# Eight chunks in four pairs: rescheduling a graph product and moving weight masks to GpSimd

## The chip, the core and the metric

The kernel runs on one core of a Trainium2 chip. The metric is the device time of one execution in microseconds (us); before the change three runs took 2383.52 to 2384.42, median 2384.4. Everything is computed in float32.

Five engines matter here: PE (TensorE, matrix products into PSUM), DVE (VectorE), ACT (ScalarE), POOL (GpSimd) and SP, which only issues DMAs. Each engine works through its own instructions in the order in which the program text gives them to it (the kernel runs under a manual schedule). An instruction that waits holds back all that stand behind it on its engine.

## What is computed

For each of 16 samples, layer 0 builds a weight matrix from the layer-normed sample, multiplies the sample with it (the graph product), and uses the result as queries of an attention. Layer 1 multiplies with a fixed normalised adjacency and applies two linear layers with batch norms.

```
h = max(layernorm(x), 0)                      # (16, 1024, 256)
A_s = 2*| |sigmoid(c_m - c_n) - 0.5| - 0.5 |  # c: channel mean of each node
g = relu((h^T @ (adj * A_s)) * para)          # graph product, 256 x 1024
k, v = split(h @ kv_w)
x = x + softmax(g^T k * scale) v              # 4 heads of 64
h = max(layernorm(x), 0)
agg = A_hat @ h;  z = relu(BN(agg @ W1.T + b1));  x = x + BN(z @ W2.T + b2)
```

The weight matrix is made from `1 - tanh(|.|)`: the kernel forms `w = (tanh(|row - col|) - 1) * adj` and puts the sign into a later scale.

## The kernel before

**Tiles.** The 1024 nodes of a sample are eight chunks of 128; each chunk `c` has a weight tile `ws[b, c]` of 128 x 1024. `differences(b, c)` (L349) makes its absolute value and tanh on ACT (L353, L356); `masked(b, c)` (L359) subtracts 1 and multiplies by `adj_t[c]` on DVE in one instruction (L361). The tiles come from pools: `w4` has five, `pp` has eight with the tag `p` (probabilities, and between attentions loaded tiles) and two with the tag `acc`, and `ow` has one each of the tags `sums` and `att`. A new tile of a full pool waits until its predecessor has been read for the last time.

**A sample's period.** For samples 2 to 15 the order is: attention of sample b (`attention`, L791), graph product and keys and values of sample b+1 (`graph_seven`, L501), then layer 1's first product of sample b (`linear1_all`). Samples 0 and 1 use the plain `graph` (L384).

**Attention.** Four steps, two heads over 512 queries each. In step s, `scores(s)` issues sixteen score products, eight exponentials on ACT and, on DVE, running sums of the probabilities (`acc`, `odd`; L816, L822, L825); then the steps in `before_last`, then the last sum (L830). `partial(s)` transposes and reduces the sum on DVE (L836, L844), and `values(s)` multiplies with `v` and transposes the output into `oT` (L865). The `hooks` fill `before_last`: in steps 0 and 1 the weight tiles 0 and 1 of the next sample. After `partial(2)`, `scale` of the first half (two of the four steps) multiplies `oT` by the reciprocals (L903), and SP issues sixteen DMAs (L920) that lay it out in the tile `att`. `add` (L928) adds `att` to half of the sample `x` on DVE. For the first half this call, `add0`, stands late in the graph product; the second half's `collect`, `invert`, `spread`, `scale`, `add1` are spread over the graph product and what follows.

**Graph product.** `graph_seven` treats chunks 0 and 1 plainly (`plain`, four block products of 128 x 128 by 128 x 512 for each chunk, L514) and the other six in three pairs. A pair's 2 x 2 by 2 x 2 block product takes seven products (`m1` to `m_7`, L575) instead of eight, with sums s1 to s4 of blocks of h on the left (made beforehand by `pair_sums`, stored by POOL's DMA queue, loaded again by SP at L527 and L528) and differences t1 to t4 of weight tiles on the right (`make_t1` to `make_t4`, one DVE instruction of 128 x 512 each, L556 to L568). The sum of several products stands in one PSUM tile `x` that is copied out three times in between (L642, L654, L659). t2 and t3 use the still empty `v` and `kT` tiles.

**Loads.** At the head of `graph_seven` SP loads the sums, h transposed (L532), `para` (L535) and, by `load_more`, the six tiles of the three adjacency differences that `linear1` reads (L982).

Of the kernel before, what the change touches and what calls it, by code (L numbers as in the profile page):

```python
# [10 lines left out]
F32 = mybir.dt.float32  # L11
# [6 lines left out]
P = 128  # L18
# [11 lines left out]
def fast_path(  # L30
# [37 lines left out]
    gs_d = [dram.tile([P, 12, P], F32, tag=f"fgs_{b}", name=f"fgs_{b}") for b in range(B)]  # L68
# [107 lines left out]
    with ExitStack() as stage:  # L176
# [181 lines left out]

        def masked(b, c):  # L359
            w = ws[b, c]  # L360
            nc.vector.scalar_tensor_tensor(w, w, 1.0, adj_t[c], ALU.subtract, ALU.mult)  # L361
# [100 lines left out]
        PLAIN = 2  # L462
        PAIRS = (NC - PLAIN) // 2

        def h_pairs(b, n0, n1):

            view = hs[b][:, PLAIN + 2 * n0 : PLAIN + 2 * n1, :].rearrange(
                "p (n k) c -> p n k c", k=2
            )
            return lambda i, k: view[:, :, k, ts(i, P)]  # L470
# [30 lines left out]
        def graph_seven(b, left, norm, load_more, last):  # L501
# [5 lines left out]
            add0, collect, invert, spread, scale, add1 = left  # L507
            h = hs[b]

            def plain(c):  # L510
                w = ws.pop((b, c))
                for d in range(CC):
                    for g in range(NH):
                        nc.tensor.matmul(  # L514
                            gps[d][:, ts(g, 512)],
                            h[:, c, ts(d, P)],
                            w[:, ts(g, 512)],
                            start=(c == 0),
                            stop=(c == PLAIN - 1),
                        )  # L520


            w7 = pp.tile([P, N], F32, tag="acc", name=f"f_w_{b}_7", bufs=2)
            rest = pp.tile([P, 2, 512], F32, tag="acc", name=f"f_kt4_{b}", bufs=2)
            sums_h = ow.tile([P, 4, 2, P], F32, tag="sums", name=f"f_gs_{b}")
            sums_c = rest[:, 0].rearrange("p (s q) -> p s q", s=4)
            nc.sync.dma_start(sums_h, gs_d[b][:, 0:8].rearrange("p (s n) q -> p s n q", s=4))  # L527
            nc.sync.dma_start(sums_c, gs_d[b][:, 8:12])  # L528
# [7 lines left out]
            load_more()  # L536
# [6 lines left out]
            def s_of(q):  # L543
                return [sums_h[:, q, n] for n in range(2)] + [sums_c[:, q]]
# [3 lines left out]
            def part_w(n, k, j):  # L548
                return ws[b, PLAIN + 2 * n + k][:, ts(j, 512)]

            t2 = [diffs[:, 2 * n] for n in range(2)] + [room[:, 3]]
            t3 = [diffs[:, 2 * n + 1] for n in range(2)] + [room[:, 1]]
# [34 lines left out]
            def m2(n):  # L587
                one(c_of[0, 0], a(0, 1)[:, n], part_w(n, 1, 0), n)

            def m3(n):  # L590
                one(c_of[0, 1], s4[n], part_w(n, 1, 1), n)

            def m4(n):
                one(c_of[1, 0], a(1, 1)[:, n], t4[n], n)
# [10 lines left out]
            differences(b, 2)  # L605
            differences(b, 3)
            differences(b, 4)
            masked(b, 2)
            masked(b, 3)
            collect()  # L610
            invert()
            masked(b, 4)
            plain(0)
            differences(b, 5)
            make_t3(0)
            make_t1(0)
            make_t2(0)
            spread()
            masked(b, 5)
            plain(1)  # L620
            differences(b, 6)
            differences(b, 7, w7)
            m1(0)
            m2(0)
            make_t4(0)
            m3(0)
            m_7(0)
            m1(1)
            make_t3(1)
            masked(b, 6)  # L630
            m2(1)
            m4(0)
            m_7(1)
            m3(1)
            make_t1(1)
            make_t2(1)
            sums = big.tile([P, 2, 4, P], F32, tag="row", name=f"f_kvs_{b}")
            nc.sync.dma_start(sums.rearrange("p m n q -> p (m n) q"), kvs_d)
            scale()
            masked(b, 7)  # L640
            m1(2)
            nc.scalar.copy(room[:, 0], x)  # L642
# [3 lines left out]
            m2(2)  # L646
            m6(0)
            m6(1)
            make_t4(1)
            make_t4(2)  # L650
            m_7(2)
            m3(2)
            m6(2)
            nc.scalar.copy(room[:, 2], x)  # L654
            m4(1)
            m4(2)
# [3 lines left out]
            add0()  # L660
# [3 lines left out]
            t23 = ow.tile([P, 2, 512], F32, tag="att", name=f"f_kt23_{b}")  # L664
            kt2, kt3, kt4 = t23[:, 0], t23[:, 1], rest[:, 1]
# [9 lines left out]
            for d in range(CC):  # L675
                nc.vector.tensor_add(both(d), both(d), gps[d])
            for c in range(PLAIN, NC):
                ws.pop((b, c))
# [69 lines left out]
            arrive(b + 1)  # L748
            V.add(1, 0, 7)
# [41 lines left out]
        def attention(b, qT, kT, v, hooks):  # L791
# [4 lines left out]
            def scores(s, within=None, before_last=()):  # L796
                g, pair = steps[s]
                for m in range(NC):
                    ps = ps_s.tile([P, 2, 512], F32, tag="s", name=f"f_s_{b}_{s}_{m}")
                    for e in range(2):  # L800
                        rows_e = slice(e * HD, (e + 1) * HD)
                        nc.tensor.matmul(  # L802
                            ps[:, e, :],
                            kT[rows_e, pair, ts(m, P)],
                            qT[rows_e, pair, ts(g, 512)],
                            start=True,
                            stop=True,
                        )
                    p = pp.tile([P, 2, 512], F32, tag="p", name=f"f_p_{b}_{s}_{m}")
                    nc.scalar.activation(p, ps, AF.Exp)  # L810
                    p_of[s, m] = p
                    if m == 1:
                        acc = pp.tile(
                            [P, 2, 512], F32, tag="acc", name=f"f_acc_{b}_{s}", bufs=2
                        )
                        nc.vector.tensor_add(acc, p_of[s, 0], p)  # L816
                        acc_of[s] = acc
                    elif m == 3:
                        odd = ow.tile([P, 2, 16, 32], F32, tag="sums", name=f"f_sums_{b}_{s}")
                        odd_of[s] = odd  # L820
                        flat = odd.rearrange("p e j i -> p e (j i)")
                        nc.vector.tensor_add(flat, p_of[s, 2], p)  # L822
                    elif m > 3:
                        to = flat if m % 2 else acc_of[s]
                        nc.vector.tensor_add(to, to, p)  # L825
                    if m == 5 and within:
                        within()
                for step in before_last:
                    step()
                nc.vector.tensor_add(acc_of[s], acc_of[s], flat)  # L830

# [104 lines left out]
            for i in range(len(steps)):  # L936
                scores(
                    i,
                    collect if i == 2 else None,
                    [*hooks.get(i, ()), *([invert, spread] if i == 2 else [])],  # L940
                )
                partial(i)
                if i == 2:
                    scale()
                values(i)
            return [add] + finish(1)
# [31 lines left out]
        def load_thirds(b):  # L978
            made = [third_tiles(b, k) for k in range(3)]
            for k in range(3):  # L980
                for i in range(KH // 2):
                    nc.sync.dma_start(made[k][i], t_d[k][:, 2 * i : 2 * i + 2, :])  # L982
            return made
# [382 lines left out]
        with tc.manual_schedule(engines={ENG.PE, ENG.Activation, ENG.DVE, ENG.Pool, ENG.SP}):  # L1366
# [73 lines left out]
            for b in range(B):  # L1440

                hooks = {}
                if b + 1 < B:
                    for c in range(2):
                        hooks.setdefault(c, []).append(lambda c=c: weights(b + 1, c))
# [8 lines left out]
                left = attention(b, *qkv, hooks)  # L1454

                def more(c):
# [5 lines left out]
                        lambda: turn_h(b + 1), more(2), left[0], left[1], left[2], more(3),  # L1462
                        left[3], left[4], more(4),
# [4 lines left out]
                    4: [left[5], lambda: norm.stats(4, NC), norm.invert],  # L1468
# [8 lines left out]
                if b + 1 < B:  # L1477
                    more_loads = {}

                    def load_more():  # L1480
                        if 0 < b < B - 2:
                            more_loads["thirds"] = load_thirds(b)

                    if b == 0:
                        qkv = graph(b + 1, between)
                        todo = []
                    else:
                        qkv, todo = graph_seven(b + 1, left, norm, load_more, b + 2 == B)
                        thirds = more_loads.get("thirds")
# [4 lines left out]
                if b + 2 < B:  # L1494
                    made = None
                    if b > 0:
# [9 lines left out]
                        turning=lambda: (pair_sums(b + 2, 2, 3), turn_h_aside(b + 2)),  # L1506
# [5 lines left out]
                else:  # L1512
# [3 lines left out]
                    def first():  # L1516
                        norm.stats(0, 4)
                        norm.invert(0, 4)
                        left[3]()
                        left[4]()  # L1520
# [5 lines left out]
                    def third():  # L1526
                        left[5]()
# [17 lines left out]
                    for step in left[:3]:  # L1545
                        step()
# [897 lines left out]
```

## Time and profile before

The page describes one execution: its own time is 2382.97 us, of which 2381.1 are the span from first to last instruction.

| | before |
|---|---|
| median of three runs | 2384.4 us |
| the profiled execution | 2382.97 us |
| its span | 2381.1 us |
| PE busy | 2343.5 us, 98% |
| DVE busy | 1989.6 us, 84% |
| ACT busy | 1352.6 us, 57% |
| POOL busy | 175.1 us, 7% |
| granted PE clock, mean | 0.995 |
| one period (attention, graph product, layer 1), from the scores at 1111.45 to those at 1241.98 | 130.5 us |

Busy time is the union of an engine's instructions. A group line reads: line, engine, operation, output <- inputs, shapes, count | busy us, mean ns of one | idle time just before and what ended it. A float32 product appears as two PE records, and each record's own duration (592 ns) overlaps the next one's, so that PE advances faster than the mean suggests. The timeline merges neighbours: start in us, duration, engine, line, operation, count. Inside the loop PE is never idle by these records; its idle time lies at the start and at the end.

### The profile page before, as it was taken

How to read it: one execution, taken by the hardware profiler on the slowest of the kernel's cores; microseconds unless marked ns; L12 is line 12 of the kernel's file. 1: busy time of each engine (PE TensorE's matmuls, PEld its weight loads, DVE VectorE, ACT ScalarE, POOL GpSimd, SP SyncE). 2: the span in 40 equal slices, each digit the busy share in tenths (PEclk: the TensorE clock that was granted, in tenths of full speed). 3: DMA queues.
4: the chain of work that ended last, by engine and by line, in shares of the span. 5: the costliest groups of instructions: out<-in, count | busy, mean ns of one | idle time of the engine just before them, and what ended most of it. 6: DMA issues, size and time to landing. Idle time of an engine off the chain costs nothing.

```text
span 2381.1 us, 25131 instructions
## 1 busy us (share of the span) xinstructions
PE 2343.5 (98%) x8286; PEld 1037.3 (44%) x8286; DVE 1989.6 (84%) x2866; ACT 1352.6 (57%) x2002; POOL 175.1 (7%) x253
## 2 busy tenths in 40 slices
PE   8999999999999999999999999999999999999996
PEld 4443444434343434444343434344444434444444
DVE  6888989797989899897979798998979798757766
ACT  6846556464746555565647374555555575346654
POOL 2030010101010000101010100001010100000000
PEclk9999999999999999999999999999999999999998
DMA  5043433432342424334333414243433321355569
GB/s 194 8 145 93 147 119 129 137 122 91 97 160 68 167 93 169 97 129 137 124 98 110 146 62 169 89 172 93 146 120 127 114 92 53 114 203 188 175 238 381
DMA packets 178651, 316.40 MB, mean 133 GB/s; under 512 B 33616, under 2 KB 117072, under 8 KB 178512
## 3 DMA queue, kind: packets, MB, share of 16 engines
q1 hardware_dynamic: 164176, 271.18, 33.7%
q0 software_dynamic: 9728, 26.76, 3.8%
q10 hardware_dynamic: 4608, 16.78, 1.7%
q8 instruction: 67, 1.10, 0.2%
q14 instruction: 72, 0.59, 0.1%
HBM read 198.71 MB, written 97.05 MB: 124 GB/s over the span
## 4 chain that ended last, share of the span: by engine, by line
PE 97%; DVE 1%; DMA 1%; ACT 0%; issue 0%; SPq 0%; DVEq 0%; ACTq 0%; POOLq 0%; POOL 0%
PE f_s L802 19%; PE f_o L852 19%; PE f_aps L1011 16%; PE f_zps L1118 6%; PE f_gps L575 6%; PE f_gpsx L575 5%; PE f_gps L514 4%; PE f_zx L1661 4%; PE f_zm L1661 3%; PE f_gps L404 2%; PE f_kpsx L712 2%; PE f_vpsx L717 2%; PE f_vps L717 2%; PE f_kps L712 1%; PE f_z2ps L1599 1%; PE f_outps L1884 1%
## 5 line engine op out<-in xcount | busy, mean ns | idle before, releaser
L810 ACT ACTIVATE f_p<-f_s 128x1024 f32<-128x1024 f32 x512 | 477.5, 1048 | 189.2 <-PE f_s L802 189.1
L802 PE MATMUL f_s<-f_qT,f_kT 64*128 64x512 f32 x2048 | 457.3, 596 | 0.1
L852 PE MATMUL f_o<-f_p,f_v 128*64 128x512 f32 x2048 | 453.6, 595 | 0.0
L802 PEld LDWEIGHTS f_s<-f_qT,f_kT 64*128 64x128 f32 x2048 | 190.2, 185 | 264.8 <-ACT f_p L810 117.9
L852 PEld LDWEIGHTS f_o<-f_p,f_v 128*64 128x64 f32 x2048 | 141.4, 137 | 304.3 <-issue 265.4
L353 ACT ACTIVATE f_w<-f_row,f_col 128x1024 f32<-128x1024 f32 x127 | 147.0, 1157 | 40.0 <-PE f_gps L514 26.8
L825 DVE TENSOR_TENSOR f_acc<-f_acc,f_p 128x1024 f32<-128x1024 f32 x128 | 155.9, 1218 | 4.5 <-ACT f_p L810 4.5
L361 DVE SCALAR_TENSOR_TENSOR f_w<-f_w,f_adj 128x1024 f32<-128x1024 f32 x127 | 152.8, 1213 | 7.5 <-ACT f_w L356 7.2
L825 DVE TENSOR_TENSOR f_sums<-f_sums,f_p 128x1024 f32<-128x1024 f32 x128 | 155.8, 1217 | 0.0
L260 POOL TENSOR_TENSOR f_rstd_b<-f_var_b,f_mhalf 128x4 f32<-128x4 f32 (+1 forms) x31 | 33.1, 1069 | 1483.0 <-DVE f_var_b L259 1483.0
L356 ACT ACTIVATE f_w<-f_w 128x1024 f32<-128x1024 f32 x127 | 134.4, 1058 | 4.0
L1011 PE MATMUL f_aps<-f_ahatT,f_hs 128*128 128x512 f32 x256 | 115.1, 592 | 0.0
L1011 PE MATMUL f_aps<-f_ahatT,f_h_b 128*128 128x512 f32 x256 | 112.7, 593 | 0.0
L1011 PE MATMUL f_aps<-f_t,f_hs 128*128 128x512 f32 x256 | 112.5, 592 | 0.0
L816 DVE TENSOR_TENSOR f_acc<-f_p,f_p 128x1024 f32<-128x1024 f32 x64 | 76.9, 1201 | 27.6 <-ACT f_p L810 27.5
L514 PE MATMUL f_gps<-f_w,f_h_a 128*128 128x512 f32 x224 | 99.9, 599 | 0.0
L822 DVE TENSOR_TENSOR f_sums<-f_p,f_p 128x1024 f32<-128x1024 f32 x64 | 78.3, 1223 | 21.8 <-ACT f_p L810 21.8
L281 ACT ACTIVATE f_h_a<-f_x,f_shift_a,f_rstd_a 128x256 f32<-128x256 f32 x126 | 73.8, 587 | 38.5 <-DVE f_shift_a L266 38.5
L836 DVE STREAM_TRANSPOSE f_sums<-f_acc 128x1024 f32<-128x1024 f32 x64 | 79.7, 1245 | 2.2
L281 ACT ACTIVATE f_h_b<-f_x,f_shift_b,f_rstd_b 128x256 f32<-128x256 f32 x128 | 69.3, 595 | 21.5 <-DVE f_shift_b L266 21.5
L575 PE MATMUL f_gps<-f_w,f_h_a 128*128 128x512 f32 x168 | 81.2, 592 | 0.0
L1141 ACT ACTIVATE f_z<-f_zps,f_b 128x512 f32<-128x512 f32 x60 | 38.0, 683 | 75.3 <-PE f_zps L1118 75.3
(285 smaller groups left out, 3754.0 us busy)
## 6 DMA issues: line engine op xcount, KB each, us to landing
f_t<-ft SPq DMA_DIRECT2D x84, 512.0 KB, 11.1
fz<-f_z SPq DMA_DIRECT2D x64, 512.0 KB, 9.7
f_x<-in_x_dram SPq DMA_DIRECT2D x31, 1024.0 KB, 7.0
f_zb<-fz SPq DMA_DIRECT2D x42, 512.0 KB, 3.9
f_att<-f_oT SPq DMA_DIRECT2D x512, 32.0 KB, 1.9
fx<-f_x SPq DMA_DIRECT2D x16, 1024.0 KB, 4.4
fhT<-f_hQ POOLq DMA_DIRECT2D x112, 128.0 KB, 2.9
f_hT<-fhT SPq DMA_DIRECT2D x28, 512.0 KB, 5.9
```

Of the source, the lines that this page charges most:

```text
L281: nc.scalar.activation(self.h[:, c, :], self.xt[:, c, :], AF.Relu, bias=self.shift[:, c : c + 1], scale=self.rstd[:, c : c + 1], accum_out ...
L353: nc.scalar.activation(w, rows[b], AF.Abs, bias=cols[b][:, c : c + 1], scale=0.5 / C)
L361: nc.vector.scalar_tensor_tensor(w, w, 1.0, adj_t[c], ALU.subtract, ALU.mult)
L514: nc.tensor.matmul(gps[d][:, ts(g, 512)], h[:, c, ts(d, P)], w[:, ts(g, 512)], start=(c == 0), stop=(c == PLAIN - 1),)
L575: nc.tensor.matmul(ps, left, right, start=fresh and n == 0, stop=(n == PAIRS - 1), skip_group_check=more,)
L802: nc.tensor.matmul(ps[:, e, :], kT[rows_e, pair, ts(m, P)], qT[rows_e, pair, ts(g, 512)], start=True, stop=True,)
L810: nc.scalar.activation(p, ps, AF.Exp)
L825: nc.vector.tensor_add(to, to, p)
L852: nc.tensor.matmul(o_of[s][e * HD : (e + 1) * HD, :], v[:, m, ts(2 * pair + e, HD)], p[:, e, :], start=(m == 0), stop=(m == NC - 1),)
L1011: nc.tensor.matmul(ps, left[:, m, :], right(m), start=not more and m == 0, stop=(m == KH - 1), skip_group_check=more,)
L1118: nc.tensor.matmul(ps[i], left[:, ts(i, P)], right, start=not more, stop=True, skip_group_check=more,)
L1661: nc.tensor.matmul(ps, left[:, m, :], right[:, m, :], start=start and m == 0, stop=(m == 1), skip_group_check=not start,)
```

## The change

It touches `graph_seven`, the attention loop, and the loads.

- All eight chunks form four pairs; `plain` is gone. The order of the products, of the t's and of the masks in the graph product is written anew, with the six products m1, m2, m3 of the pairs 0 and 1 first.
- The weight tiles 0 to 3 of the samples 2 to 15 are made in the attention steps 0 to 3: `differences` in `before_last`, then, after the step's last sum, `masked_aside`: DVE writes a column of -1, ACT adds it to the tile (Identity with that column as bias), and GpSimd multiplies by `adj_t[c]`.
- `add` of the first half stands in attention step 3, ahead of the hooks and of the step's last sum. This holds for all 16 samples.
- `sums_h` takes the tag `att`, `t23` the tag `sums`, `kt4` a tile of its own.
- The third adjacency difference is loaded later, behind the load of the next sample; `pair_sums` of the second part makes two pairs instead of one.

```diff
+        def masked_aside(b, c):
+            now = small.tile([P, 1], F32, tag="now", name=f"f_now_{b}_{c}")
+            nc.vector.memset(now, -1.0)
+            w = ws[b, c]
+            nc.scalar.activation(w, w, AF.Identity, bias=now)
+            nc.gpsimd.tensor_mul(w, w, adj_t[c])
...
-        PLAIN = 2
-        PAIRS = (NC - PLAIN) // 2
+        PAIRS = NC // 2
...
-            add0, collect, invert, spread, scale, add1 = left
+            collect, invert, spread, scale, add1 = left
...
-            sums_h = ow.tile([P, 4, 2, P], F32, tag="sums", name=f"f_gs_{b}")
+            sums_h = ow.tile([P, 4, 2, P], F32, tag="att", name=f"f_gs_{b}")
...
-            load_more()
+            load_more(0, 2)
...
-            differences(b, 2)
-            differences(b, 3)
-            differences(b, 4)
-            masked(b, 2)
-            masked(b, 3)
+            for n in range(2):
+                m1(n)
+            for n in range(2):
+                m2(n)
+            for n in range(2):
+                m3(n)
+            differences(b, 4, w4th)
+            differences(b, 5, w5th)
             collect()
...
+            differences(b, 6, later[0])
+            differences(b, 7, later[1])
...
+            for n in range(2):
+                make_t3(n)
+                make_t1(n)
+                make_t2(n)
+            make_t4(0)
+            make_t4(1)
+            masked(b, 4)
+            masked(b, 5)
+            masked(b, 6)
+            m_7(0)
+            m_7(1)
+            m4(0)
+            m4(1)
             m1(2)
+            m2(2)
+            m1(3)
             nc.scalar.copy(room[:, 0], x)
             make_t3(2)
             make_t1(2)
             make_t2(2)
-            m2(2)
+            masked(b, 7)
+            m_7(2)
+            m3(2)
             m6(0)
             m6(1)
+            m2(3)
+            invert()
+            spread()
             make_t4(2)
+            make_t3(3)
+            make_t1(3)
+            make_t2(3)
+            make_t4(3)
+            scale()
+            m3(3)
+            m4(2)
             m6(2)
+            m_7(3)
+            m6(3)
             nc.scalar.copy(room[:, 2], x)
+            m4(3)
             for n in range(PAIRS):
                 m5(n)
             nc.scalar.copy(room[:, 1], x)
-            add0()
...
             arrive(b + 1)
+            load_more(2, 3)
...
-            def scores(s, within=None, before_last=()):
+            def scores(s, within=None, before_last=(), after_last=()):
...
                 nc.vector.tensor_add(acc_of[s], acc_of[s], flat)
+                for step in after_last:
+                    step()
...
-                    [*hooks.get(i, ()), *([invert, spread] if i == 2 else [])],
+                    [
+                        *([add] if i == 3 else []),
+                        *hooks.get(i, ()),
+                        *([invert, spread] if i == 2 else []),
+                    ],
+                    aside.get(i, ()),
...
-                    for c in range(2):
-                        hooks.setdefault(c, []).append(lambda c=c: weights(b + 1, c))
+                    for c in range(2 if b == 0 else 4):
+                        if b == 0:
+                            hooks.setdefault(c, []).append(lambda c=c: weights(b + 1, c))
+                            continue
+                        hooks.setdefault(c, []).append(lambda c=c: differences(b + 1, c))
+                        aside[c] = [lambda c=c: masked_aside(b + 1, c)]
```

## Prediction

> **What bounds the kernel.** I read the chain of waits first, then PE's groups, then the timeline of one period (the sample whose fourth attention step starts at 1153.71), engine by engine.
>
> ```profile
> PE 97%; DVE 1%; DMA 1%; ACT 0%; issue 0%; SPq 0%; DVEq 0%; ACTq 0%; POOLq 0%; POOL 0%
> ...
> L514 PE MATMUL f_gps<-f_w,f_h_a 128*128 128x512 f32 x224 | 99.9, 599 | 0.0
> ...
> L575 PE MATMUL f_gps<-f_w,f_h_a 128*128 128x512 f32 x168 | 81.2, 592 | 0.0
> ```
>
> PE is the chain. So a product removed is time gained, and any wait put before PE is time lost in full. L514 has 224 records for 14 samples x 8 products, two records a product. In the timeline consecutive products start 0.857 us apart (1175.02, 1175.88, 1176.74).
>
> **What is gained.** Per sample 8 + 21 = 29 products become 28: 0.86 us, 14 x 0.86 = 12 us. The graph product now spans 1168.05 to 1193.13, 25.1 us. One stall stands in it: the copy at L642 holds the next product for 0.65 us where 0.24 is usual, 0.4 a sample. The new order covers that copy with m_7(2) and m3(2), but the second copy is now covered by m4(3) alone, as the first was by m2(2): 0.4 back, net nothing.
>
> **The moved add.** DVE's and SP's part of the period, attention step 3:
>
> ```profile
> 1155.61 1.22 DVE L903 TENSOR_TENSOR f_oT<-f_oT,f_recs 128x1024 f32<-128x1024 f32 x1
> ...
> 1163.59 1.22 DVE L825 TENSOR_TENSOR f_sums<-f_sums,f_p 128x1024 f32<-128x1024 f32 x1
> 1164.84 1.22 DVE L830 TENSOR_TENSOR f_acc<-f_acc,f_sums 128x1024 f32<-128x1024 f32 x1
> ```
>
> ```profile
> 1156.85 10.18 SPq L920 DMA_DIRECT2D f_att<-f_oT  x16
> ```
>
> ```profile
> 1161.04 7.09 PE L852 MATMUL f_o<-f_p,f_v 128*64 128x512 f32 x32
> 1168.05 7.13 PE L514 MATMUL f_gps<-f_w,f_h_a 128*128 128x512 f32 x16
> ```
>
> `add` is put between the instructions at 1163.59 and 1164.84, but SP is still issuing the sixteen DMAs that fill `att` until 1167.0. How long after that the add can run is shown by the last sample, where it already follows the attention directly:
>
> ```profile
> 2033.44 10.63 SPq L920 DMA_DIRECT2D f_att<-f_oT  x16
> ...
> 2045.75 1.23 DVE L928 TENSOR_TENSOR f_x<-f_x,f_att 128x1024 f32<-128x1024 f32 x1 [0.27 <-issue]
> ```
>
> DVE stood idle 0.27 us before it: it ran when `att` had landed, 12.31 us after the first issue, or 1.68 after the issuing ended. Here: 1156.85 + 10.18 + 1.68 = 1168.7. So DVE, ready at 1164.8, waits 3.9 us. Behind it on DVE stand the last sum, the column of -1 for tile 3, the transpose, the reduction, the output's transpose and all t's of the graph product. ACT's Identity for tile 3 waits for that column, GpSimd's mask for ACT, and PE's fourth product, m2(1), reads tile 3.
>
> **GpSimd's mask.** No row shows a 128x1024 product there; the nearest are eight times smaller and strided:
>
> ```profile
> L1333 POOL TENSOR_TENSOR f_unused_d<-f_ahatT,f_ident 128x128 f32<-128x128 f32 x8 | 4.8, 594 | 17.9 <-ACT f_unused_r L1320 17.9
> L1334 POOL TENSOR_TENSOR f_ahatT<-f_ahatT,f_ident 128x128 f32<-128x128 f32 x8 | 4.5, 562 | 0.6
> ```
>
> Ends: 1.2 us (DVE's own time at L361) and 8 x 0.56 = 4.5. The Trainium skill, GPSIMD Engine Reference, section 3.1, gives 4497 ns for a two-input add of 2048 elements. A line through that and 0.56 us at 128 gives an estimate of 2.4 us at 1024; I take it.
>
> **Does it block DVE?** In steps 0 and 1 the mask lies beside DVE's transposes and reduction, and DVE is relieved of L361 (1.2 us each); PE gains nothing there, since it doesn't wait on DVE. In step 2 the mask starts at 1153.16 (end of the last sum) + 0.1 + 1.06 (Identity, from L356) = 1154.4 and ends at 1156.8, across L903, which reads two SBUF tensors and starts at 1155.61. The row: GpSimd's power at 1189.61 lasts to 1190.64, and DVE's L667, with two SBUF inputs, starts in it at 1190.26 and takes its usual 0.68. The rule: the Trainium skill, SBUF — State Buffer, section "Who interferes with whom", says that such a DVE instruction and a GpSimd instruction reading SBUF take a shared port as an exclusive lock. By the row L903 isn't held; by the rule it, and with it the landing of `att`, slips 1.2 us. The power reads 4 elements a partition and may be done with reading early, so I take the rule and keep the row as the low case.
>
> **The sum for one sample**, by the rule:
> - `att` landed 1169.9; add to 1171.0; last sum ends 1172.3 (1.14 us from start to start); column 0.1; Identity to 1173.45; mask to 1175.9. PE, free for m2(1) at 1168.05 + 3 x 0.857 = 1170.6, starts it at 1175.95: a stall of 5.3.
> - A gap like this has a second price. After an idle gap of 2.89 us, sixteen transposes took 3.95 us where 2.13 is usual, at a granted clock of 0.54 to 0.72:
>
> ```profile
> 2329.92 2.13 PE L1884 MATMUL f_outps<-f_ident,f_z 128*128 128x128 f32 x16 [0.85 <-DVE f_x1t L1925]
> 2334.94 3.95 PE L1884 MATMUL f_outps<-f_ident,f_z 128*128 128x128 f32 x16 [2.89 <-ACT f_z L1864]
> ```
>
>   I take two products at half speed, +1.7 us: m2(1), m3(0), m3(1), m_7(0), m_7(1) end at 1181.9.
> - DVE goes on at 1172.35 with transpose, reduction, output (1.25 + 1.25 + 0.65), and the t's from 1175.9, 0.72 + 0.72 + 0.61 for each triple, 0.65 for each t4: t4(0) at 1180.7, masks 4, 5, 6 at 1182.5, 1183.6, 1184.8. PE's m4(0) to m1(3) follow without a gap and end at 1186.2. Without the slow clock PE would meet DVE and end at 1185.7; so the clock costs only 0.5.
> - Fifteen products are left: 15 x 0.857 + 0.4 = 13.3, end at 1199.5 instead of 1193.13: **+6.3 us a sample**, the gain included; by the row +5.2.
>
> ACT is no bound: the Identities of steps 0 to 2 end 0.7 us or more before the next exponentials. Tiles 4 to 7 are made from 1173.5 on, tile 6 by 1181.1. `sums_h` waits for the add (`att`), lands 3.6 us after it (the group's median) and isn't last for m3(0). After the product: `scale` ends at 1193.9 (7 us later than before counted against PE's place), its DMAs at 10.2 + 1.7 let add1 run at about 1205.9, 6.4 after the product's end; before it ran 6.7 after. Hidden, with nothing to spare: at the slower issue of 13.05 us seen there before, add1 comes 3 us later and K's product 4, which waits for the V sums behind it, up to 2 us. The third difference is issued 15 us after the product's end behind the sample's load; 11 us of landing leave 3 to its reader at 29.9. `pair_sums` of one more pair costs 0.6 us of DVE and 256 KB on POOL's queue, in front of L1110, whose first reader has 2 us.
>
> **Two samples more.** Sample 0: `att` at 110.27 + 10.88 + 1.7 = 122.8, DVE ready at 117.9; the turned h and mask 2 then end at 132.2, while chunk 2 is due at 121.23 + 6.9 = 128.1: 4 us. Sample 15: add at 2045.75 now precedes the sum's tail; L996 ends at 2054.5 for a product due at 2051.3: 3.3. With some slow clock, 8 together.
>
> **Sum:** 14 x 6.3 + 8 = 96 on the profiled execution's 2383 (span 2381.1): 2479. The median shown lies 1.4 higher, within the error.
>
> **Rivals.**
> 1. *No lock* (the row is right, the rest as above): 14 x 5.2 + 8 = 81, 2464. For: L667. Against: its partner is tiny.
> 2. *Faster:* `att` lands before DVE asks. For tile 3 to be in time, the add may start at 1164.5 at the latest; then only the product counts: -12, 2371. Against: SP issues one every 0.64 us throughout, in each sample looked at; sixteen can't be out before 1166. It decides only if the add does not hold what follows.
> 3. *GpSimd as the bound:* the mask takes 4.5 us and locks. L903 slips 3.3, the stall becomes 9.5, the sample +10.6: 2383 + 148 + 8 = 2539. For: eight times the strided row. Against: these rows hold a fixed part and strides.
> 4. *DVE alone:* a mask as fast as DVE's (1.2), no lock, full clock: PE still meets DVE's late t4 and masks, +4.3 a sample: 2451.
>
> **How the numbers follow.** Forecast 50%, rival 1 25%, rival 3 8%, rival 4 8%, rival 2 7%, absorbed elsewhere to within 0.2% (what a measurement of this kernel can tell from no change) 2%. The range 2440 to 2515 holds the forecast and rivals 1 and 4 with their late add1; outside are rivals 2 and most of 3.
>
> **What would show it.** L928 in step 3 with DVE idle some 4 us before it, until SP's DMAs; PE idle 4 to 6 us before L575's fourth product of each sample, released by POOL; clock dips once a period; a POOL group of 56 masks near 2.4 us; L903 late by 1.2 in step 2 (lock) or not. PE without gaps at the head of the graph product would prove it wrong.

## The result, and the profile after

| | before | after |
|---|---|---|
| median of five runs on one chip | 2384.28 us | 2490.79 us |
| the runs | 2383.52 to 2384.42 | 2490.29 to 2493.61 |
| span of the profiled execution | 2381.1 us | 2489.9 us |
| granted PE clock, mean | 0.995 | 0.978 |
| graph product, mean of 14 samples | 25.08 us | 31.81 us |

The change makes the kernel slower: ratio 1.045, 95% interval 1.0436 to 1.0464, 106.5 us. The lines below are from the page of the changed kernel: busy time, the chain of waits, and three groups. In `after`, L366 is GpSimd's mask, L930 the add, L365 the Identity that subtracts 1, L572 a product of the graph product, L905 the scale.

```profile
PE 2370.0 (95%) x8258; PEld 1046.5 (42%) x8258; DVE 1985.5 (80%) x2922; ACT 1419.7 (57%) x2058; POOL 304.8 (12%) x309
...
PE 75%; DVE 8%; SPq 6%; ACT 5%; issue 2%; DMA 2%; POOL 1%; DVEq 0%; ACTq 0%; POOLq 0%
...
L366 POOL TENSOR_TENSOR f_w<-f_w,f_adj 128x1024 f32<-128x1024 f32 x56 | 132.0, 2357 | 869.3 <-ACT f_w L365 732.4
...
L572 PE MATMUL f_gps<-f_w,f_h_a 128*128 128x512 f32 x224 | 126.7, 660 | 74.8 <-POOL f_w L366 74.8
...
L930 DVE TENSOR_TENSOR f_x<-f_x,f_att 128x1024 f32<-128x1024 f32 x32 | 39.1, 1222 | 75.2 <-DMA f_att<-f_oT 74.6
```

PE was 97% of the chain and is 75%; VectorE, SP's queue, ScalarE and DMA have come in. The three groups are one story read backwards: PE stands 74.8 us before products that read tile 3, GpSimd waits for ScalarE's Identity, and VectorE's add stands 74.6 us for the DMAs of `att`. Busy time of PE rises by 26 us although it has fewer products to do: a group's mean of 660 ns, where 592 to 599 was usual, is the slow clock.

One sample, engine by engine. First PE's timeline of `after` (start, us from first start to last end, then the group; in brackets the idle time ahead and what ended it):

```profile
1221.21 1.98 PE L572 MATMUL f_gpsx<-f_w,f_h_a 128*128 128x512 f32 x4
1223.03 1.02 PE L572 MATMUL f_gps<-f_w,f_h_a 128*128 128x512 f32 x2
1229.05 2.08 PE L572 MATMUL f_gps<-f_w,f_h_a 128*128 128x512 f32 x2 [5.00 <-POOL f_w L366]
1230.92 3.16 PE L572 MATMUL f_gps<-f_w,f_gs 128*128 128x512 f32 x4
1233.91 1.88 PE L572 MATMUL f_gps<-f_v,f_gs 128*128 128x512 f32 x4
```

Three products, then 5.00 us of nothing, then three products (six records) that take 1229.05 to 1233.91, 4.86 us instead of 3 x 0.857 = 2.57. The table by windows has this stretch (length, busy time and instructions of PE, PEld, DVE, ACT and POOL, then the granted clock, the DMA share and GB/s): a clock of 0.54.

```profile
1228.90:1233.90 5.00, 4.85 (x6) 2.04 (x7) 4.86 (x8) 4.88 (x8) 0.09 (x1) 0.54 1.02 415
```

VectorE's timeline of the same sample in `after`:

```profile
1209.02 2.34 DVE L905 TENSOR_TENSOR f_oT<-f_oT,f_recs 128x1024 f32<-128x1024 f32 x1
...
1217.55 1.21 DVE L825 TENSOR_TENSOR f_sums<-f_sums,f_p 128x1024 f32<-128x1024 f32 x1
...
1222.93 1.22 DVE L930 TENSOR_TENSOR f_x<-f_x,f_att 128x1024 f32<-128x1024 f32 x1 [4.17 <-DMA f_att<-f_oT]
1224.07 1.22 DVE L830 TENSOR_TENSOR f_acc<-f_acc,f_sums 128x1024 f32<-128x1024 f32 x1
1225.24 0.06 DVE L363 MEMSET f_now<- 128x1 f32 x1
```

The scale takes 2.34 us where it took 1.22. The add waits 4.17 us, and behind it stand the last sum and the column of -1. From the column the chain runs over ScalarE (Identity 1225.41 to 1226.56) to GpSimd, whose timeline in `after` has the two masks of this stretch, the first beside the scale, the second ahead of PE's fourth product:

```profile
1207.91 2.36 POOL L366 TENSOR_TENSOR f_w<-f_w,f_adj 128x1024 f32<-128x1024 f32 x1 [13.19 <-ACT f_w L365]
1226.63 2.36 POOL L366 TENSOR_TENSOR f_w<-f_w,f_adj 128x1024 f32<-128x1024 f32 x1 [16.37 <-ACT f_w L365]
```

Where the time lies over the whole run, from the starts of the scores of each sample: the 14 samples with `graph_seven` +94.3 us (6.73 each), sample 0 +6.75, sample 15's tail +7.3; with +0.5 ahead of the first scores that is the spans' difference of 108.8.

### The profile page after: what moved, and what is told of

Its sections match the earlier page's. It is cut to its first block, busy times and chain, and to the rows that moved or that the text cites. A ratio compares the mean times of both kernels' runs of the same rounds, so it can differ in the third digit from the quotient of the medians.

```text
span 2489.9 us, 25147 instructions
## 1 busy us (share of the span) xinstructions
PE 2370.0 (95%) x8258; PEld 1046.5 (42%) x8258; DVE 1985.5 (80%) x2922; ACT 1419.7 (57%) x2058; POOL 304.8 (12%) x309
## 4 chain that ended last, share of the span: by engine, by line
PE 75%; DVE 8%; SPq 6%; ACT 5%; issue 2%; DMA 2%; POOL 1%; DVEq 0%; ACTq 0%; POOLq 0%
PE f_aps L1018 15%; PE f_s L802 10%; PE f_o L854 9%; PE f_gps L572 9%; PE f_zps L1125 6%; SPq L922 5%; PE f_gpsx L572 5%; ACT f_p L810 4%; PE f_zx L1672 4%; PE f_zm L1672 3%; PE f_kpsx L711 2%; PE f_vpsx L716 2%; PE f_gps L413 2%; PE f_vps L716 2%; PE f_kps L711 1%
## 5 line engine op out<-in xcount | busy, mean ns | idle before, releaser
L366 POOL TENSOR_TENSOR f_w<-f_w,f_adj 128x1024 f32<-128x1024 f32 x56 | 132.0, 2357 | 869.3 <-ACT f_w L365 732.4
L572 PE MATMUL f_gps<-f_w,f_h_a 128*128 128x512 f32 x224 | 126.7, 660 | 74.8 <-POOL f_w L366 74.8
L365 ACT ACTIVATE f_w<-f_w,f_now 128x1024 f32<-128x1024 f32 x56 | 64.3, 1148 | 162.2 <-DVE f_now L363 162.1
L572 PEld LDWEIGHTS f_gps<-f_w,f_h_a 128*128 128x128 f32 x224 | 44.1, 204 | 133.3 <-POOL f_w L366 86.4
L930 DVE TENSOR_TENSOR f_x<-f_x,f_att 128x1024 f32<-128x1024 f32 x32 | 39.1, 1222 | 75.2 <-DMA f_att<-f_oT 74.6
L370 DVE SCALAR_TENSOR_TENSOR f_w<-f_w,f_adj 128x1024 f32<-128x1024 f32 x71 | 84.0, 1216 | 3.8 <-ACT f_w L356 3.8
```

The source lines that it names most:

```text
L366: nc.gpsimd.tensor_mul(w, w, adj_t[c])
L572: nc.tensor.matmul(ps, left, right, start=fresh and n == 0, stop=(n == PAIRS - 1), skip_group_check=more,)
```

## The experiments

The theory is the prediction's: the add waits for DMAs that SP is still issuing, the chain behind it ends in tile 3's mask, and GpSimd's mask of tile 2, which holds the scale through a shared lock, makes `att` later still; a slow clock follows each gap. The rivals: the new order of the products or VectorE's load is at fault and not the add's place; GpSimd's length decides; the lock does not exist. Ten kernels tell these apart; the last four also look for a version that beats both kernels.

**The add put back** (add_back): the first half's add stands again behind the product's last copy, and two tiles change their tags with it.

```diff
-                        *([add] if i == 3 else []),
...
+            add0()
             norm.stats(0, 4)
...
-            sums_h = ow.tile([P, 4, 2, P], F32, tag="att", ...)
+            sums_h = ow.tile([P, 4, 2, P], F32, tag="sums", ...)
-            t23 = ow.tile([P, 2, 512], F32, tag="sums", ...)
+            t23 = ow.tile([P, 2, 512], F32, tag="att", ...)
```

> The changed kernel with the add of the first half back at its old place behind the last copy of the graph product, and the tags sums and att exchanged back; GpSimd still masks four tiles, the four pairs stay. My theory (the add, waiting for its sixteen DMAs in step 3, holds the column for tile 3 and all that follows): PE no longer waits for GpSimd at the fourth product; what is left is a wait for s4, because sums_h now waits for the reduction (1.4 us behind the product's start, 3.6 us of landing, due at 3.4): 1.6 us at m3(0). Graph product 26.1 us, 1.0 more than before, 2398 us (2388 to 2408). Rival (GpSimd's mask or the new order is slow in itself): GpSimd's wait stays at several us a sample, above 2450.

Measured: 2411.85 us, ratio to before 1.0122 (1.0105 to 1.0139); 78.9 us of the 106.5 are gone. PE no longer waits for GpSimd at all, but a new wait stands in the list of PE's waits of this kernel (us in total, times, longest):

```profile
PE f_gps L572 <- DMA f_gs<-fgs: 26.0, 14, 2.3
```

1.86 us a sample for the sums of h, and the slow clock behind it in five samples of 14 (product 28.1 to 28.5 us there, 25.9 to 26.6 elsewhere). The wait itself was expected (1.6 us); the slow clock behind it was not, and so the total lies above the expected 2388 to 2408. The load of `sums_h` waits for its tile, which the reduction of step 3 reads: in one sample SP had issued the scale's sixteen transfers by 1180.62, the reduction ended at 1181.61, and the load went out at 1181.64. In `after` the longer stall had covered this.

**The add behind the values** (add_after_values): the add stays in attention step 3, but behind `values(3)`, so that nothing of tile 3 stands behind it.

```diff
-                        *([add] if i == 3 else []),
...
                 values(i)
+                if i == 3:
+                    add()
```

> As the run before, but the add stands behind the output's transpose of step 3, ahead of the first difference. The DMAs have landed or nearly so by then, so it costs DVE 1.15 us and no wait worth speaking of. Theory: the t's move 0.75 us and stay behind PE's wait for s4: the same 2398 us within 6. Rival (DVE is the bound at the head of the product, every us counts): 14 x 0.75 = 10 us more than the run before, 2408.

Measured: 2413.8 us, ratio 1.0124 (1.0107 to 1.0141), the product 27.05 us against 27.00 in add_back. The 2 us between the two lie within the intervals: the add as such costs nothing in this place that these runs can tell; what costs is what is queued behind it.

**The add moved alone** (add_alone): the kernel before, with nothing but the add moved into step 3.

```diff
                     [
+                        *([add] if i == 3 else []),
                         *hooks.get(i, ()),
...
-            return [add] + finish(1)
+            return [lambda: None] + finish(1)
```

> The kernel before with one part of the change alone: the add of the first half stands in step 3, ahead of the last sum; masks, products and tiles as before. Theory: DVE waits 3.9 us there and is 1.1 later by the add itself; the graph product's weights stand behind it on DVE, PE waits for the masks of tiles 2, 3, 5 and 7 in turn, and the last of them (due at 15.6 us, now at 20.5) sets the loss: 4.5 us a sample and some 7 in the samples 0 and 15, 70 us, 2454 (2435 to 2475). Rival (it needs GpSimd's mask behind the add): the eight plain products hide it, under 2400.

Measured: 2463.92 us, ratio 1.0338 (1.0321 to 1.0356), +80.8 us against before; the product 30.02 us. GpSimd masks nothing here; PE waits for VectorE's masks (26.9 + 9.1 us) and differences (15.6) instead, and the add waits 71.0 us for `att`. So the moved add alone makes three quarters of the loss, with either product and with either maker of the tiles, and GpSimd is merely the last link where it makes tile 3.

**Tiles 2 and 3 without GpSimd's product** (no_mask_2, no_mask_3).

```diff
-            nc.gpsimd.tensor_mul(w, w, adj_t[c])
+            if c != 2:
+                nc.gpsimd.tensor_mul(w, w, adj_t[c])
```

> The changed kernel without GpSimd's multiplication of weight tile 2 (left out: that tile is not multiplied by adj). Lock theory (GpSimd's mask holds the scale instruction of step 2, which then holds the sixteen DMAs, the add and tile 3): the scale takes 1.22 us instead of 2.34, the add starts 1.1 us earlier, and so does everything: 14 x 1.1 = 15 us less than the changed kernel, 2475. Without that chain: 2490, unchanged.

> The changed kernel without GpSimd's multiplication of weight tile 3 (left out: that tile is not multiplied by adj). If GpSimd's 2.36 us were simply on the path, 14 x 2.4 = 33 us would go: 2457. My ledger has DVE's differences and masks right behind: PE starts m2(1) 2.4 us earlier, then waits for t4 and the masks of tiles 4 to 6, which are freed by the lock alone (0.5 us): 0.9 us a sample, 13 us, 2478.

Both took some 6780 us as a whole. With the unmultiplied tile the kernel's own test of the ranges sends it to its general path after the fast one; so neither total can be read, and only the fast path's part of the trace is used. VectorE's timeline of no_mask_2 in one sample (L906 is the scale, L931 the add):

```profile
1201.32 1.21 DVE L906 TENSOR_TENSOR f_oT<-f_oT,f_recs 128x1024 f32<-128x1024 f32 x1
...
1214.14 1.22 DVE L931 TENSOR_TENSOR f_x<-f_x,f_att 128x1024 f32<-128x1024 f32 x1 [3.98 <-DMA f_att<-f_oT]
```

and PE's:

```profile
1220.26 2.07 PE L573 MATMUL f_gps<-f_w,f_h_a 128*128 128x512 f32 x2 [3.91 <-POOL f_w L367]
```

Without GpSimd beside it the scale takes 1.21 us and not 2.34; the add begins 0.63 us after the product's start (at 1213.51 here) and not 1.72, and PE's wait is 3.91 and not 5.00: 1.1 us all the way through. The lock is there and its effect is passed on in full in this sample; over all 14 PE's waits fall from 74.8 to 61.2 us, 0.97 each. The product gains less, 31.81 to 31.05 us on the mean; in this sample the slow clock lasted longer, 0.56 over the 6.3 us behind the gap. Without tile 3's mask the product's mean is 30.52: 1.3 us less, not the mask's 2.36; how the rest divides between the clock and VectorE's late differences was not separated.

**The clock** (warm): the changed kernel with five idle products ahead of the wait, into a half of PSUM that nothing has used yet.

```diff
-            for n in range(2):
-                m2(n)
+            m2(0)
+            for n in range(5):
+                nc.tensor.matmul(gps[1][:, 512:1024], a(0, 1)[:, 0], part_w(0, 1, 0), start=True, stop=True)
+            m2(1)
```

> The changed kernel with five idle products (m2(0)'s operands, into the half of a PSUM tile that nothing reads) between m2(0) and m2(1): they fill 4.3 of the 5.3 us in which PE waits for GpSimd, so that the clock need not fall. Nothing else moves. The prediction's ledger put the slow clock at 0.5 us a sample behind DVE's lag: then 14 x 0.5 = 7 us less than the changed kernel, 2484. By the changed kernel's own trace (graph product 31.8 us; at full clock PE would meet t4(0) at 12.4, the masks of tiles 4 to 6 at 14.2, 15.3, 16.5 and end at 30.6): 14 x 1.2 = 17 us, 2474. Without any effect of the clock: 2490.

Measured: 2478.99 us, ratio to before 1.0399 (1.0382 to 1.0416), 11.8 us less than the changed kernel, or 0.84 us a sample. PE's remaining wait is 1.60 us in one sample, and the clock behind it 1.00 where it was 0.54. The late tile comes no earlier here: the fourth product begins 8.41 us after the first on the mean, in `after` 8.19. From there to the product's end it takes 22.59 us and not 23.63. So the slow clock's own price is 1.04 us a sample, of which a tile some 0.2 us later gives back a part; the rest of the slow clock's duration runs beside VectorE's lag.

**The sums loaded earlier** (sums_early): add_back with two tiles exchanged, so that `sums_h` need not wait for the tile of step 3's sums.

```diff
-            w5th = pp.tile([P, N], F32, tag="acc", ...)
-            sums_h = ow.tile([P, 4, 2, P], F32, tag="sums", ...)
+            w5th = ow.tile([P, N], F32, tag="sums", ...)
+            sums_h = pp.tile([P, 4, 2, P], F32, tag="acc", ...)
```

> The run with the add back, and sums_h and w5th exchange their places: sums_h goes to a tile that is free since step 3 began, so that its load need not wait for the reduction and lands some 2.6 us behind the product's start, due at 3.4. The wait for s4 (26 us in all there) and the slow clock behind it go. Left are waits of PE for DVE's t4 and masks of 0.3 to 0.4 us each, some 1.1 a sample: graph product 25.5 us against 25.1 before: 2390 (2382 to 2396). If the wait for s4 was hidden anyway: 2410.

Measured: 2394.59 us, ratio 1.0048 (1.0031 to 1.0064). PE's wait for the sums falls from 26.0 to 16.0 us and no further, and the clock stays at 1.00 in all 14 products. SP's timeline of this kernel says why:

```profile
1162.98 10.47 SPq L923 DMA_DIRECT2D f_att<-f_oT  x16
1173.56 0.51 SPq L523 DMA_DIRECT2D f_gs<-fgs  x1
```

The tile is free, but SP issues in order: sixteen transfers of `att` first, until 0.64 us after the product's start at 1172.81.

**Another order** (reordered): sums_early with the masks of tiles 4 to 6 ahead of the second differences on VectorE, and PE's products in the matching order.

```diff
-            for n in range(2):
-                make_t3(n)
-                make_t1(n)
-                make_t2(n)
-            make_t4(0)
-            make_t4(1)
+            make_t3(0)
+            make_t3(1)
             masked(b, 4)
             masked(b, 5)
             masked(b, 6)
...
+            make_t1(0)
+            make_t2(0)
+            make_t4(0)
+            masked(b, 7)
```

> As sums_early, with DVE's and PE's order in the product written for DVE's times: t3 of two pairs, masks 4 to 6, then the other differences; m1 and m2 of pair 2 and m1(3) run before m4. By the ledger PE then waits 0.1 us a sample, and the product takes 24.4 us instead of 25.1: 14 x 0.7 = 10 us less than the kernel before, 2374 (2368 to 2383), faster than both kernels. If the add, now late again on DVE, delays keys and values: 2385 to 2395.

Missed: 2415.56 us, ratio 1.0139 (1.0122 to 1.0156), slower than sums_early. VectorE's timeline has the reason:

```profile
1186.20 2.35 DVE L370 SCALAR_TENSOR_TENSOR f_w<-f_w,f_adj 128x1024 f32<-128x1024 f32 x2
1190.36 1.22 DVE L370 SCALAR_TENSOR_TENSOR f_w<-f_w,f_adj 128x1024 f32<-128x1024 f32 x1 [1.82 <-ACT f_w L356]
```

Tile 6's mask now comes before ScalarE has made the tile: VectorE stands for 1.82 us, and every difference moved behind the mask is that much later. The product takes 26.67 us on the mean and not 25.68, which makes 14 of the 21 us lost against sums_early; the others lie behind the product and were not traced to a cause. Of the two orders the one that the change had chosen is the better.

**The sums on GpSimd's queue** (own_queue): sums_early with one word changed.

```diff
-            nc.sync.dma_start(sums_h, ...)
+            nc.gpsimd.dma_start(sums_h, ...)
```

> The kernel of sums_early with one word changed: the load of sums_h (L523) is issued by GpSimd's queue, which has nothing but its four weight tiles to do, and no longer by SP's, where it stood behind the scale's sixteen transfers and went out 0.75 us after the product had begun. Nothing is left out. If the 1.14 us a sample for which the PE waited for f_gs in sums_early is SP's order alone: that wait (16.0 us over 14 samples) goes to under 1 us in all. Not all of it comes back, because VectorE was hidden behind it: t4(1) then ends at +7.8 us of the product and the weight tiles 4 to 6 at +8.9, +10.0 and +11.2, where the PE would stand for them at +8.1, +9.0, +9.8 and +10.7; so 0.4 to 0.6 us of waiting for VectorE takes its place. Product 25.0 to 25.3 us (25.68 in sums_early, 25.08 before), gain 0.4 to 0.7 us a sample with 15 samples, total 2386 (2381 to 2390). Rival 1, the whole 1.14 us is gained and the remaining slow clock with it: 2374 to 2380. Rival 2, what held the load is not SP's order but the transfers' own landing among the sixteen: f_gs lands as late as before, total 2393 to 2397.

Missed by far: 2502.1 us, ratio 1.0497 (1.0483 to 1.0511), the slowest of the kernels that leave nothing out. GpSimd's timeline:

```profile
1225.34 2.37 POOL L366 TENSOR_TENSOR f_w<-f_w,f_adj 128x1024 f32<-128x1024 f32 x1 [11.10 <-ACT f_w L365]
1227.65 0.60 POOL L523 DMA_DIRECT2D f_gs<-fgs  x1
```

SP's timeline:

```profile
1215.35 10.20 SPq L923 DMA_DIRECT2D f_att<-f_oT  x16
1225.71 0.46 SPq L525 DMA_DIRECT2D f_gsr<-fgs  x1
1226.42 0.88 SPq L529 DMA_DIRECT2D f_hT<-fhT  x2
1227.35 0.42 SPq L532 DMA_DIRECT2D f_qT<-in_L_gnn_para_dram  x1
```

and PE's:

```profile
1236.54 3.78 PE L572 MATMUL f_gps<-f_w,f_gs 128*128 128x512 f32 x4 [7.65 <-DMA f_gs<-fgs]
1240.12 2.94 PE L572 MATMUL f_gps<-f_v,f_gs 128*128 128x512 f32 x4
```

The expectation took GpSimd's queue for empty. It is not: the load stands in program order behind tile 3's mask, which waits for ScalarE, and is issued at 1227.65, 2.46 us after the product's start. By then SP's other loads, of 512 KB and 1 MB each, are out, and `f_gs` takes 8.0 us to land in the median, where it takes 3.6 in ahead_of_scale. The queue changed, and the place in time got worse; no other experiment makes the dependence on the place so plain.

**The sums ahead of the scale** (ahead_of_scale): sums_early with the load and the scale written into step 3's scores, the load first.

```diff
                         acc_of[s] = acc
+                        if s == 3 and 0 < b < B - 1:
+                            t = pp.tile([P, 4, 2, P], F32, tag="acc", ...)
+                            nc.sync.dma_start(t, gs_d[b + 1][:, 0:8]...)
+                            early_of[b + 1] = t
+                            scale()
+                        nc.vector.tensor_add(acc, p_of[s, 0], p)
...
-                if i == 2:
+                if i == 2 and not 0 < b < B - 1:
                     scale()
```

> The kernel of sums_early with the load of sums_h put on SP's queue ahead of the scale's sixteen transfers: it is written inside the scores of attention step 3, behind the allocation of that step's running sum (so that its tile still takes the buffer that step 2 has freed), and the scale follows it there, behind the transpose of step 2's values and ahead of step 3's first addition. So the scale also begins some 1 us later, behind most of GpSimd's mask of tile 2. Nothing is left out. own_queue has shown that the load's place decides: issued 2.45 us after the product began, behind SP's larger loads, f_gs came 7.65 us late. If so, here it is issued some 12 us ahead of the product and the PE's wait for f_gs (16.0 us over 14 samples in sums_early) is gone; VectorE's lag behind it leaves 0.4 to 0.6 us a sample. Product 25.0 to 25.3 us (25.68 in sums_early), total 2386 (2380 to 2390): within half a per cent of before, on either side. Rival 1, the whole 1.14 us and the slow clock's rest come back: product 24.2 to 24.5, total 2372 to 2380, faster than before. Rival 2, the later scale delays step 3's additions (0.9 us of VectorE idle time ahead of them is all the room there is) and with them the mask of tile 3 and the product's first differences: total 2390 to 2400.

Measured: 2379.99 us, ratio 0.9985 (0.9978 to 0.9991), 3.6 us below the 2383.6 of before on the same chip. It is the only kernel of the study that beats before, and by less than the 0.2% named in the prediction as the bound of what can be told. The edit moves two things, the load and the scale; that the load's place is what counts is read from PE's waits. Its load is issued at 1136.09, 28.9 us ahead of the product and not 12 (its tile was free earlier than the expectation had it), and PE's waits for `f_gs` are gone. PE's timeline of the whole head of the product (here L573):

```profile
1164.99 1.98 PE L573 MATMUL f_gpsx<-f_w,f_h_a 128*128 128x512 f32 x4
1166.81 1.88 PE L573 MATMUL f_gps<-f_w,f_h_a 128*128 128x512 f32 x4
1168.52 1.88 PE L573 MATMUL f_gps<-f_w,f_gs 128*128 128x512 f32 x4
1170.24 1.88 PE L573 MATMUL f_gps<-f_v,f_gs 128*128 128x512 f32 x4
1171.96 1.88 PE L573 MATMUL f_gps<-f_w,f_h_a 128*128 128x512 f32 x4
1173.67 1.02 PE L573 MATMUL f_gpsx<-f_w,f_h_a 128*128 128x512 f32 x2
1174.53 1.09 PE L573 MATMUL f_gps<-f_w,f_h_a 128*128 128x512 f32 x2
1175.63 1.12 PE L573 MATMUL f_gpsx<-f_w,f_h_a 128*128 128x512 f32 x2
1176.60 1.02 PE L573 MATMUL f_gps<-f_kT,f_gsr 128*128 128x512 f32 x2
```

No bracket and no 2.08. Where products follow at 0.857 us everywhere else, the starts of the last three are 1.10 and 0.97 apart: 0.24 + 0.11 = 0.35 us a sample for VectorE's masks of tiles 5 and 6, less than the 0.4 to 0.6 expected. The product spans 24.57 us here, 24.61 on the mean.

## Why the prediction held

The forecast was 2479 us in a range of 2440 to 2515; measured were 2490.79. The direction and the mechanism were right, and most links had the right size; the slow clock's price was put too low, and part of the agreement is luck, as the sums below show.

| step of the prediction | predicted | measured in `after` |
|---|---|---|
| add starts after the product's start | 1.85 us (1169.9 - 1168.05) | 2.05 mean of 14 (1.67 to 2.58; 1.72 in the sample above) |
| GpSimd's mask | 2.4 us | 2.357 mean |
| the scale slips under GpSimd's mask of tile 2 | 1.2 us | 2.34 instead of 1.22 |
| fourth product starts after the first | 7.90 us (1175.95 - 1168.05) | 8.19 mean |
| from there to the product's end | 23.55 us (1199.5 - 1175.95) | 23.63 mean |
| add1 after the product's end | 6.4 us, hidden | 6.15 to 7.18, PE has no wait there |
| one sample | +6.3 us | +6.73 |
| sample 0 | +4, without the slow clock | +4.3, with it +6.75 |
| sample 15 | +3.3, without the slow clock | +3.0, in all +7.3 |

**The lock** was a choice between a row that showed no holding and the Trainium skill's rule (SBUF — State Buffer, "Who interferes with whom"). The rule won: 2.34 us beside the mask, 1.21 in no_mask_2 without it. The scale ends at 1211.36, 1.09 us after the mask's end at 1210.27: that is what a hold until then gives, with nearly its whole usual 1.22 us still to come. It bears once more on the first difference of the product, which takes 1.17 us beside tile 3's mask where its like takes 0.67; there PE is not waiting for VectorE. Rival 1, no lock, would have given 2464 and is out.

**The wait and what is queued behind it** is the core, and it stands: add_back takes 78.9 us off, add_alone puts 80.8 on. Rival 2 (the data lands before VectorE asks) and rival 3 (a mask of 4.5 us) fell with the profile's first lines. Rival 4's late VectorE exists, as add_alone and no_mask_3 show, but hidden behind the longer chain.

**What was mis-sized.** The forecast fell 12 us short. Half of this, 6.05 us, lies in the samples 0 and 15: "With some slow clock, 8 together" was 14.05. The waits were as forecast, 4.3 and 3.0 us; for the slow clock behind them the sum has 0.7. In `after` eight records behind the wait of sample 0 and sixteen behind that of sample 15 took

```profile
132.88 6.12 PE L413 MATMUL f_gps<-f_w,f_h_a 128*128 128x512 f32 x8 [4.06 <-DVE f_w L370]
...
2155.71 10.18 PE L1018 MATMUL f_aps<-f_t,f_hs 128*128 128x512 f32 x16 [2.83 <-issue]
```

where eight take 3.60 at full clock, and the same sixteen took 7.03 in `before`:

```profile
2051.31 7.03 PE L1011 MATMUL f_aps<-f_t,f_hs 128*128 128x512 f32 x16
```

Nothing lags beside PE there, so the whole price shows: 2.5 and 3.1 us. The last 1.1 us of sample 15 lie further on and were not traced.

The other half is 0.43 us in each of 14 samples. 0.29 of it is a later tile, 0.20 of that a later add: SP took 10.18 to 11.06 us to issue the sixteen DMAs, and the prediction had reckoned with the shortest. (The profile's wait, 5.34 us on the mean, counts from the recorded end of the third product; counted as the prediction's 5.3 is, it is 5.62.) The rest is 0.08 behind the tile and 0.07 of rounding. The slow clock is not in this half, and that is luck: "so the clock costs only 0.5" was 1.04 by warm, but without it the prediction had 23.05 us from the fourth product to the end, and warm takes 22.59. Two errors of half a microsecond cancel.

**The gain of the removed product** was put at 12 us. A kernel without the stall lets it be seen: in ahead_of_scale the product goes from 25.08 to 24.57 us in twelve of 14 samples, 0.51 and not 0.86; 0.35 goes to VectorE's masks. With the two slower samples it is 6.6 us in all. Of these the span keeps 3.2: in the profiled executions 0.6 us goes ahead of the first scores, 0.6 between the first and the last and 2.2 behind those. What takes them was not tried.

The prediction didn't see the load of `sums_h`. It said of it that it "isn't last for m3(0)", which is right in `after` and only because tile 3 is later still. Taken one after another, the medians leave this account of the 106.5 us: the add's place 78.9 (to add_back), the tile that `sums_h` waits for 17.3 (to sums_early), its place on SP, with the scale's, 14.6 (to ahead_of_scale), and -3.6 to -4.3 for all the rest, by which of the runs of before one counts. The kernels ran on different chips, on which the medians of before differ by up to 1.1 us.

## What to carry to other kernels

Before an instruction is moved up, ask when its data lands and not whether its engine is free, and then list what is queued behind it on that engine and who waits for those: here an add of 1.2 us cost 80 because tiles of the next product stood behind it. When a stall is removed, the next late thing is one that it had covered, so look at every load issued in the same stretch, and put a small load with an early reader ahead of the many small transfers on its queue; another queue helps only if the place in its program order is earlier too. Count a wait of some 2 us or more before PE as more than its length, since the clock can fall behind it; where another engine lags beside PE, part of that price is hidden.

## What the runs showed that was not expected

- The granted clock fell behind waits much shorter than expected, and not behind all of the same length. In add_back PE waits 1.44 to 2.29 us at the same place of 14 samples; the four records behind the wait, 1.98 us in nine of them, took 2.48 to 3.68 in five: behind waits of 1.89, 1.93, 2.12, 2.22 and 2.29 us, but not behind one of 2.06.
- What decides is where a wait lies. The granted clock is 1.0 or 0.5 in all twelve traces (values between are means over a stretch), and in each trace it falls and comes back only on a grid of 3.413 us. Here are two pairs of neighbouring windows of this grid in add_back, around the wait of 2.06 us and around that of 1.93 (length, busy time and records of PE, granted clock, DMA share, GB/s):

```profile
785.29:788.70 3.41, 2.02 (x5) 1.00 0.70 208
788.70:792.12 3.42, 2.74 (x7) 1.00 1.03 407
1710.30:1713.71 3.41, 1.47 (x4) 1.00 0.92 274
1713.72:1717.13 3.41, 3.41 (x4) 0.50 1.03 417
```

  The longer wait is spread over two windows and leaves PE busy for 59% and 80% of them. The shorter one lies in a single window and leaves 43%, and the next window runs at half clock. Between 30 and 2360 us of the twelve traces there are 8069 windows at full clock. All 82 of them with PE busy below 42% were followed by half clock, and none above 45%; of the nine between these limits three were. By these figures a single wait below 0.55 x 3.41 = 1.88 us does not lower the clock. The Trainium skill (TensorE: Matmul & The Clock Gate, "Part 1: The HAM clock gate") gives a window of 3413 ns that does not start with the kernel, and half clock after an idle one. The length agrees with the traces, but here a window did not have to be idle.
- How long the clock stays low follows from the same grid. A window at half clock was followed by full clock only when PE was busy for 82% of it or more. The clock was low for two windows in the sample of `after`, for two in that of no_mask_2 and for three in that of own_queue; what was left of them when the wait ended, 4.4, 5.5 and 5.7 us, is what PE paid for.
- A 512 KB load took 3.6 us in the median on SP's queue ahead of the sixteen small transfers and 8.0 in the median when issued by GpSimd behind SP's large loads; that queue and moment both changed, so their shares are not told apart.
